# Graph attention of the last layer with nodes on partitions: row sums from ACT, squares crossed from SBUF to SBUF

## The chip, the cores and the metric

The kernel runs on one core of one Trainium2 chip. The metric is the device time of one execution in microseconds (us). Engines are named as in the profile: PE (TensorE matmul), PEld (its weight loads), DVE (VectorE), ACT (ScalarE), POOL (GpSimd), SP (SyncE, which issues nearly all DMAs).

## What is computed

The input x has 32 graphs of 512 nodes with 256 channels; all share one 512x512 adjacency. Four layers run in a row, each as x = x + layer(relu(layernorm(x))): two dense-and-attention blocks (layer 0), a graph attention with self loops (layer 1), a masked multi-head attention of 8 heads with two layer norms (layer 2), and the graph attention that this change is about (layer 3), of 4 heads with 64 channels:

```python
q = (h @ W).reshape(B, N, H, D)
e_src = jnp.einsum('bnhd,d->bnh', q, a_src)
e_dst = jnp.einsum('bnhd,d->bnh', q, a_dst)
e = e_src[:, :, None, :] + e_dst[:, None, :, :]
e = jnp.where(e >= 0, e, ALPHA * e)              # ALPHA = 0.2
e = jnp.where((adj > 0)[None, :, :, None], e, NEG_INF)
attn = jax.nn.softmax(e, axis=2)
h_prime = jnp.einsum('bijh,bjhd->bihd', attn, q)
return jax.nn.elu(h_prime.reshape(B, N, H * D))
```

A node without any neighbour gets equal weights on all nodes, so its result is the mean over all nodes.

## The kernel before

All numbers are float32. A graph's array of 512 nodes and 256 channels lies as 128 partitions x 4 blocks x 256 (a "cell", 32 of which stand in SBUF); its turned form has the channels on partitions. Up to six graphs are in flight (IN_FLIGHT), and their steps are interleaved.

The order is made when the program is built. Every step is an `Op` with an engine, an assumed length, and the buffers that it reads and writes; `Plan.order` places all steps of all graphs one by one, on each engine the step that is due first among those that can start, and hands out cells, PSUM banks, rows, pages and sheets as it goes. A step's due time comes from the rest of its graph's chain, a period per graph (PERIOD) and one number per step (SHIFTS). The result is one fixed order of instructions on each engine and on SP's DMA queue; at run time semaphores hold each instruction until its data are there, and what stands behind it on the same engine waits with it.

Layer 2 (`mha`) has nodes on partitions while it makes probabilities: PE makes scores (L1347), DVE adds the mask and takes the extreme of each row (L1367), ACT makes exponentials and their sums (L1378 with its accumulator read), DVE turns every 32x32 square in place (L1386), and the squares are then exchanged between the four groups of 32 partitions by a trip through DRAM: one store of 128 partitions to a "sheet" (L1391), four loads that each land on 32 partitions (L1399). `turned_round` turns the input of layers 0 and 2 in the same way through a "page" (`crossed`, L615 and L622; squares on DVE, L636). `transposed` (L655 on PE, L663 on ACT) turns it with PE for layers 1 and 3 and after the first norm of layer 2.

Layer 3 has the nodes that are summed over on partitions from the start (`layer3`, from L1450). For each of four heads, one after the other, `gat_probabilities` (L776) spreads three columns into rows with PE transposes of a broadcast column against the identity (`rows_ps`, L720): the neighbours' terms for the masked maximum (DVE, L791, into a scratch tile `masked`), a shift per node (four small operations on POOL, L806 to L809, and a copy on ACT, L730), and the nodes' own terms. POOL adds the shift to the turned mask (L821, two of 128x1024), DVE takes the larger of the two slopes and adds (L832), ACT makes the exponentials (L840). The leaky slope is thus a maximum on DVE, not a function on ACT. POOL adds the four blocks of probabilities (L1484, L1488), PE multiplies them with q (L1502, two heads side by side in 64 columns each), a matrix of ones makes the sums (L1523), PE turns rows back (L1539), DVE scales (L1548 to L1561). `lonely` and `spread` add the mean for nodes without neighbours (L851, L859, L870, L1572). `elu_to_xt` applies elu, fetches the residual from a page (L973) and adds it (L1222). One store of 512 KB takes the result out (L1588).

Of the kernel before, what the change touches and what calls it, by code (L numbers as in the profile page):

```python
# [39 lines left out]
FLOOR = -(2.0**60)  # L40
TINY = 1e-30
# [3 lines left out]
CELL = NC * (C + 5)  # L45
ROW = N + 10
SMALL = 320
BUFFERS = {"cell": 32, "row": 7, "page": 48, "sheet": 12}
# [6 lines left out]
PERIOD = 50.7  # L55
# [3 lines left out]
    72, 50, 37, 26, 40, 30, 9, 57, 9, 9, 9, 9, 50, 27, -10, -39, 3, -6, 21, -19, -30, -122,  # L59
    -182, -23, -9, -33, 39, 5, -2, 1, -49, 1, 1, 0, -66, 1, 1, 1, 1, -16, 1, -38, -1, -71, -1,  # L60
    0, -23, 1, 2, -22, 1, 3, 1, -103, 1, 5, 1, -19, 1, 1, 19, 1, -26, 1, -3, 1, 1, 1, 14, 5, 0,
    1, 1, -10, 1, -2, 0, 0, 0, 1, 0, -1, 0, -1, 6, 0, -115, 19, 0, 7, -25, -6, 0, -32, -35, 0,
    68, 0, 35, 0, 93, -3, 2, 24, -51, 18, -11, 0, -7, 1, -75, 1, 1, 55, 0, 26, -26, 4, 3, 0,
    -39, -1, -162, -3, -56, -2, -13, 1, -20, -2, -37, -87, -26, -9, -7, -1, -27, -9, -52, -40,
    6, -52, -18, 0, -6, -4, 2, -5, -23, -88, 0, -14, -42, 12, -11, -1, -2, 6, -7, -10, -1, -49,
    -29, -3, -1, -23, 2, 0, -84, 10, -16, -46, -3, 7, 7, -17, 0, 0, 0, 0, -18, 0, 4, 144, 2, 0,
    -3, 0, -7, 2, -24, 27, -28, 31, -92, 47, -25, -10, 1, 0, -3, 0, 109, 0, -1, -75, -1, 0, 0,
    -3, 0, -7, -45, 0, 41, -1, 2, -7, 69, -15, -49, -3, -3, 0, 22, -97, -17, 4, -12, -9, 4, -53,
    -11, -1, -1, -5, 17, 5, 72, 47, 46, 74, 146, -16, -51, 41, -3, -13, -15, 2, 0, 1, 49, -18,
    -5, 30, 3, 4, 0, 0, -1, 0, 18, 14, -12, -32, 78, -1, 37, -82, -4, 7, -6, 0, 9, -3, -12, 9,  # L70
    0, -70, 20, 0, -10, 0, -1, 0, 23, 0, 0, -33, -10, 28, 83, 95, 37, 17, 76, -5, -36, -119,
    -25, -1, 92, 3, 0, 2, -3, 0, -24, 1, 0, -10, -5, -3, -36, -2, -46, -24, -68, 25, -10, -11,
    -13, -5, -2, -29, -22, -1, -1, -13, -2, 3, 14, 0, 0, 0, 28, 7, -83, -101, 7, 46, -9, -54,
    -46, 44, -24, 99, -5, -1, 0, 0, 75, 0, 0, 0, -10, 0, 1, 6, 0, 14, 0, 23, 13, -17, 53, 6, 87,
    -7, -16, 7, 3, 5, -1, -71, -87, 15, -12, 0, 11, 0, 0, 0, 8, 0, 0, -9, -8, 0, 23, 0, 0, -80,
    2, 0, 18, 0, 0, -3, 0, 0, 105, -13, -36, -11, -81, -30, -85, -143, -51, -24, -71, -29, -116,
    -48, -84, -82, -187, -154, -123, -175, -94, -43, -87, -62, 6, -91, -111, -160, -332, -388,
    -421, -351, -608, -395, -425, -396, -421, -341, -408, -335, -348, -464, -413, -372, -375,
    -378, -330, -297, -285, -312, -291, -315, -190, -199, -193, -90, -130, -236, -99, 76, -225,
    -189, -251, -299, -395, -387, -220, -242, -187, -183, -124, -28, -137, -109, -189, -108,  # L80
    -163, -117, -33, -55, -60, -125, -183, -244, -216, -176, -221, -264, -255, -199, -296, -271,
    -259, -434, -424, -521, -444, -340, -233, -214, -298, -180, -115, -52, -68, -145, -240,
    -205, -240, -241, -326, -236, -241, -474, -309, -46, -175, -128, -162, -177, -202, -326,
# [325 lines left out]
def adj_preln_kernel(  # L409
# [83 lines left out]
    w1_sb = weights(w1, "w1_sb")  # L493
    b1_bc = column(b1, "b1_bc")
    w2_sb = weights(w2, "w2_sb")
    l3_sb = weights(W_3, "l3_sb", TERMS * GAT_HEADS)
    ln1_g_bc = column(ln1_g, "ln1_g_bc")
    ln1_b_bc = column(ln1_b, "ln1_b_bc")
    ln1_g_row = row(ln1_g, "ln1_g_row")
# [1148 lines left out]
```

## Time and profile before

| | |
|---|---|
| time, median of 3 runs | 4420.88 us (4417.97 to 4422.98) |
| the profiled execution: time, span | 4422.42 us, 4420.6 us |
| mean granted PE clock | 0.979 |
| instructions | 69,315 |
| DMA | 867 MB, 196 GB/s over the span |
| DMAs with data, issued by SP | 2,102 |
| stores of results (L1588), start of the first, the 28th, the 32nd | 571, 4097, 4417 us |

The page lists busy time by engine, the granted clock and the DMA share in 40 slices, the chain of work that ended last, and groups of instructions by line: count, busy time in us, mean ns of one, and the idle time of the engine just before them with what ended it. A window gives the busy time of each engine in a stretch, then the granted clock, the share of the 16 DMA engines' time that packets took, and GB/s. Matmuls overlap, so a matmul's own duration is longer than the time until the next one can start.

### The profile page before, as it was taken

To read this page: it belongs to the slowest core of one execution; us is meant where nothing else is said; L and a number is where in the kernel's file an instruction comes from. 1 tells how busy PE (TensorE), PEld (TensorE's weight loads), DVE (VectorE), ACT (ScalarE), POOL (GpSimd) and SP (SyncE) were. 2 spreads that over 40 slices of the span, in tenths; PEclk is the share of its full clock that TensorE was granted. 3 is DMA by queue.
4 is the path that set the end of the run, shared out by engine and by line. 5 is a ranking of instruction groups with operands and counts; after the bars stand their busy time and mean duration, and the time that the engine had idled before them with its cause. 6 is when DMAs were issued, how large, how long until landed. Compare 5 with 4: busy or idle time off the path is not lost. (4 is left out here: it accounts for less than half of the span.)

```text
span 4420.6 us, 69315 instructions
## 1 busy us (share of the span) xinstructions
PE 4170.8 (94%) x21648; PEld 2583.3 (58%) x21648; DVE 3662.7 (83%) x9016; ACT 2924.3 (66%) x6309; POOL 3034.1 (69%) x3119
## 2 busy tenths in 40 slices
PE   6999999999999999999999999999999999999765
PEld 3656556665566666566666556666656666655332
DVE  3577888888888888888888888888889888888873
ACT  2556666777676667667667767666766766676653
POOL 1424766777776677776677777667777766777677
PEclk9999999999999999999999999999999999999877
DMA  3287667766767766766777667677667677766760
GB/s 121 84 226 218 187 190 220 218 202 181 215 199 211 224 200 201 204 204 194 222 215 204 201 200 211 194 224 210 205 205 206 192 217 219 201 200 186 231 175 29
DMA packets 441504, 867.22 MB, mean 196 GB/s; under 512 B 35248, under 2 KB 119728, under 8 KB 441136
## 3 DMA queue, kind: packets, MB, share of 16 engines
q1 hardware_dynamic: 439520, 862.78, 66.4%
q8 instruction: 173, 2.83, 0.3%
q14 instruction: 195, 1.60, 0.1%
q10 hardware_dynamic: 1616, 0.01, 0.0%
HBM read 443.23 MB, written 419.43 MB: 195 GB/s over the span
## 5 line engine op out<-in xcount | busy, mean ns | idle before, releaser
L1386 DVE STREAM_TRANSPOSE cells<-cells 128x512 f32<-128x512 f32 x1024 | 702.4, 698 | 148.8 <-ACT cells L1378 148.5
L1378 ACT ACTIVATE cells<-cells,smalls 128x512 f32<-128x512 f32 x1024 | 736.1, 719 | 114.0 <-DVE smalls L1367 105.8
L1367 DVE CUSTOM_DVE_ANT_0 cells<-bank,mask_bias 128x512 f32<-128x512 f32 x1024 | 686.9, 674 | 21.6 <-PE bank L1347 20.6
L821 POOL TENSOR_TENSOR cells<-mask_biasT,row 128x1024 f32<-128x1024 bf16 x320 | 682.3, 2155 | 16.2 <-ACT row L730 16.2
L791 DVE CUSTOM_DVE_ANT_0 masked<-bank,mask_bias 128x512 f32<-128x512 f32 x768 | 520.5, 678 | 71.1 <-PE bank L720 64.7
L683 PE MATMUL bank<-cells,mlp_sb 128*128 128x512 f32 x1024 | 473.1, 600 | 19.8 <-DMA cells<-page 13.2
L704 PE MATMUL bank<-fc_sb,cells 128*128 128x256 f32 (+1 forms) x2048 | 474.7, 381 | 1.5 <-DVE smalls L1367 0.8
L927 PE MATMUL bank<-cells 128*128 128x260 f32 x2048 | 465.1, 383 | 1.1 <-ACT cells L840 0.9
L603 ACT ACTIVATE cells<-cells,smalls 128x256 f32<-128x256 f32 x768 | 408.1, 592 | 74.7 <-POOL smalls L596 49.7
L1159 PE MATMUL bank<-cells 128*128 128x512 f32 x1024 | 450.9, 597 | 0.0
L927 PEld LDWEIGHTS bank<-cells 128*128 128x128 f32 x2048 | 387.9, 190 | 87.1 <-issue 24.9
L840 ACT ACTIVATE cells<-cells,smalls 128x512 f32<-128x512 f32 x512 | 348.5, 726 | 114.7 <-DVE cells L832 114.6
L704 PEld LDWEIGHTS bank<-fc_sb,cells 128*128 128x128 f32 x2048 | 376.9, 189 | 76.5 <-DVE cells L1442 19.0
L586 DVE BATCH_NORM_STATS2 smalls<-cells 128x6 f32<-128x256 f32 x768 | 311.3, 405 | 110.4 <-POOL cells L1222 101.3
L883 ACT ACTIVATE cells<-cells 128x512 f32<-128x512 f32 (+1 forms) x256 | 188.1, 735 | 292.9 <-DVE cells L946 111.3
L832 DVE SCALAR_TENSOR_TENSOR cells<-bank,smalls,cells 128x512 f32<-128x512 f32 x512 | 354.1, 740 | 30.5 <-POOL cells L821 27.0
L720 PEld LDWEIGHTS bank<-ident,smalls 128*128 128x128 f32 x2176 | 254.3, 141 | 212.6 <-issue 84.2
L720 PE MATMUL bank<-ident,smalls 128*128 128x128 f32 x2176 | 325.9, 284 | 54.2 <-POOL smalls L809 30.0
L1159 PEld LDWEIGHTS bank<-cells 128*128 128x128 f32 x1024 | 194.1, 193 | 230.2 <-issue 228.7
L1484 POOL TENSOR_TENSOR cells<-cells 128x1024 f32<-128x1024 f32 x128 | 302.3, 2372 | 19.2 <-PE bank L1502 8.4
L683 PEld LDWEIGHTS bank<-cells,mlp_sb 128*128 128x128 f32 x1024 | 186.0, 191 | 218.5 <-issue 170.3
L1347 PE MATMUL bank<-cells 32*128 32x512 f32 x2048 | 305.8, 644 | 5.7 <-DVE smalls L1367 4.8
(141 smaller groups left out, 8503.9 us busy)
## 6 DMA issues: line engine op xcount, KB each, us to landing
sheet<-cells SPq DMA_DIRECT2D x256, 1024.0 KB, 5.3
cells<-sheet SPq DMA_DIRECT2D x1024, 256.0 KB, 5.4
page<-cells SPq DMA_DIRECT2D x256, 512.0 KB, 3.4
cells<-page SPq DMA_DIRECT2D x192, 512.0 KB, 6.1
cells<-in_x_dram SPq DMA_DIRECT2D x64, 512.0 KB, 7.3
cells<-page SPq DMA_DIRECT2D x256, 128.0 KB, 2.9
out_dram<-cells SPq DMA_DIRECT2D x32, 512.0 KB, 5.4
mlp_sb<-in_L_gnn_mlp_w_dram SPq DMA_DIRECT2D x2, 512.0 KB, 6.7
```

The source lines that it names most:

```text
L603: lambda c=c: act.activation(xn[:, c, :], src[:, c, :], func, bias=off[:, c : c + 1], scale=rstd[:, c : c + 1],),
L683: lambda k=k, s=s, i=i, m=m, mm=mm: pe.matmul(mm.ap, w[:, k, cols + m * P : cols + (m + 1) * P], s.rows(i), start=(k == 0), stop=(k == nk ...
L704: pe.matmul(mm[:, :n], src[k // 2].nodes(k % 2, c), w[:, k, cols : cols + n], start=(k == 0), stop=(k == nk - 1),)
L720: pe.transpose(bc[:, c * P : (c + 1) * P], col(c).to_broadcast([P, P]), ident)
L791: lambda c=c: dve.tensor_tensor_reduce(masked, f2_ps.ap, bias[:, c, :], 1.0 - ALPHA, FLOOR, op0=ALU.add, op1=ALU.max, accum_out=top[:, c : ...
L821: lambda half=half: pool.tensor_add(p[half].ap, biasT[:, 2 * half : 2 * half + 2, :], w_row[:, None, :].to_broadcast([P, 2, N]),),
L832: lambda j=j, ph=ph, i=i: dve.scalar_tensor_tensor(ph[:, i, :], f1_ps.ap, term(2)[:, j : j + 1], ph[:, i, :], op0=ALU.max, op1=ALU.add,),
L927: pe.matmul(mm[:, :w1], p[j // 2][:, j % 2, c * P : (c + 1) * P], v[:, j, :], start=(j == 0), stop=(j == NC - 1),)
L1159: pe.matmul(mm.ap, h1[jh][:, i, m * P : (m + 1) * P], p[jh][:, i, :], start=(jh + i == 0), stop=(jh + i == 2),)
L1367: dve.tensor_tensor_reduce(tile(), sc[h].ap.rearrange("p (j f) -> p j f", j=NC), mask_bias[:, c, :].rearrange("p (j f) -> p j f", j=NC), - ...
L1378: lambda h=h, c=c, tile=tile: act.activation(tile(), tile(), AF.Exp, scale=-1.0, bias=low[:, c, h : h + 1], accum_out=sums[:, c, h : h + 1],),
L1386: dve.transpose(squared, squared)
```

## The change

Layer 3 is made like layer 2's attention, with nodes on partitions until the probabilities are done. Its input is turned by DVE and a trip through a page (`turned_round`) in place of PE and ACT, which leaves the nodes in "square order" (the position of a node's block and its group of 32 are exchanged); the mask is brought into this order once at the start, and the residual and the result are moved in it by four DMAs each. One row per head is spread by PE (`square_row`). DVE adds the mask and takes row maxima (into the probabilities themselves), ACT applies the leaky slope (Prelu with the node's own term as bias) and the exponential with its row sum, DVE turns the squares in place. For two heads at a time, 16 DMAs of 128 KB exchange the squares straight from SBUF to SBUF, 32 partitions to 32 partitions; then PE multiplies in one step. The sums by POOL and PE, the turned mask's adds, the mean for nodes without neighbours and the third group of columns in the weights go. The mask's value is so large that a row without neighbours comes out with equal weights by itself.

Buffers change a little: five rows in place of seven, cells smaller by four columns, 342 small columns per graph in place of 320. Steps per graph go from 657 to 721 by the program's count (PE 132 to 117, ACT 158 to 170, POOL 57 to 37, DVE 181 to 182, DMAs 65 to 108). PERIOD and all SHIFTS are new, so the order of steps is new everywhere, not only in layer 3.

```diff
@@ constants
+LOWEST = -3.0e38
+PAIR = 2
 ...
-CELL = NC * (C + 5)
-ROW = N + 10
-SMALL = 320
-BUFFERS = {"cell": 32, "row": 7, "page": 48, "sheet": 12}
+CELL = NC * (C + 4)
+ROW = N + 8
+SMALL = 342
+BUFFERS = {"cell": 32, "row": 5, "page": 48, "sheet": 12}
-PERIOD = 50.7
+PERIOD = 52.0
 SHIFTS = (
...
 )
@@ new helpers
+        def square_row(self, holder, col, dst):
+            bc = Buffer("bank", N)
+            def emit():
+                for c in range(NC):
+                    pe.transpose(
+                        bc.ap.rearrange("p (q c i) -> p q c i", q=NC, i=SQUARE)[:, :, c, :],
+                        col(c).to_broadcast([P, P]),
+                        ident,
+                    )
+            self.op("pe", 0.47, holder, [bc, *dst], emit)
+            return bc
+        def masked_probabilities(self, holder, far, near, n, table, p, tile, parts, sums=None):
+            bias, key = table
+            f2_ps = self.square_row(holder, far, [p])
+            top = self.small(f"top{n}", NC)
+            m = self.small(f"m{n}", NC)
+            for c in range(NC):
+                self.op(
+                    "dve", 0.77, [f2_ps, [(key, c, q) for q in range(P // SQUARE)]], [top, parts(c)],
+                    lambda c=c: dve.tensor_tensor_reduce(
+                        tile(c),
+                        f2_ps.ap.rearrange("p (a i) -> p a i", i=tile(c).shape[2]),
+                        bias[:, c, :].rearrange("p (a i) -> p a i", i=tile(c).shape[2]),
+                        1.0, LOWEST,
+                        op0=ALU.add, op1=ALU.max, accum_out=top[:, c : c + 1],
+                    ),
+                )
+            self.op(
+                "pool", 0.35, [top, *holder], [top],
+                lambda: pool.tensor_add(top.ap, top.ap, near()),
+            )
+            def emit():
+                act.activation(m.ap, top.ap, AF.Prelu, alpha=ALPHA)
+                act.activation(m.ap, m.ap, AF.Copy, scale=-1.0)
+            self.op("act", 0.45, [top], [m], emit)
+            for c in range(NC):
+                self.op(
+                    "act", 0.72, [*holder, parts(c)], [parts(c)],
+                    lambda c=c: act.activation(
+                        tile(c), tile(c), AF.Prelu, bias=near()[:, c : c + 1], alpha=ALPHA
+                    ),
+                )
+            for c in range(NC):
+                def emit(c=c):
+                    out = {} if sums is None else {"accum_out": sums[0](c)}
+                    act.activation(tile(c), tile(c), AF.Exp, bias=m[:, c : c + 1], **out)
+                self.op(
+                    "act", 0.72 if sums is None else 0.82, [m, parts(c)],
+                    [parts(c), *([sums[1]] if sums else [])], emit,
+                )
+                def emit(c=c):
+                    squared = tile(c).rearrange("p a (l i) -> p a l i", i=SQUARE)
+                    dve.transpose(squared, squared)
+                self.op("dve", 0.69, [parts(c)], [parts(c)], emit)
+        def squares_crossed(self, src, dst, read, write, kbytes):
+            squares = P // SQUARE
+            for turn in range(squares):
+                for l in range(squares):
+                    to = (l + turn) % squares
+                    def emit(l=l, to=to):
+                        nc.sync.dma_start(
+                            dst(slice(to * SQUARE, (to + 1) * SQUARE), l),
+                            src(slice(l * SQUARE, (l + 1) * SQUARE), to),
+                        )
+                    self.transfer([read], write(l, to), kbytes, emit, True, 0.6)
@@ the residual, fetched in square order
+        def fetched_squares(self, page, after):
+            dst = Buffer("cell", *page.shape)
+            for q in range(P // SQUARE):
+                def emit(q=q):
+                    nc.sync.dma_start(
+                        dst[q * SQUARE : (q + 1) * SQUARE],
+                        page[:, q, :].rearrange("(c i) f -> i c f", i=SQUARE),
+                    )
+                self.transfer(
+                    [page, *after], [[(dst, "from", q)]], 128, emit, True
+                )
+            return dst
@@ share(): the mask in square order, once
+            quarters = range(P // SQUARE)
+            page = [("mask page", 0)]
+            self.transfer(
+                [[("mask", c) for c in range(NC)]], [page], 256,
+                lambda: nc.sync.dma_start(mask_page, mask_bias),
+            )
+            for q in quarters:
+                def emit(q=q):
+                    nc.sync.dma_start(
+                        mask_square[q * SQUARE : (q + 1) * SQUARE],
+                        mask_page[:, q, :].rearrange("(c i) f -> i c f", i=SQUARE),
+                    )
+                self.transfer(
+                    [page], [[("square", c, q) for c in range(NC)]], 64, emit, True
+                )
@@ the residual added
-        def add_to_xt(self, y, after):
-            xt = self.fetched(self.x_page, after)
+        def add_to_xt(self, y, after, squares=False):
+            xt = (self.fetched_squares if squares else self.fetched)(self.x_page, after)
+            landed = [(xt, "from", q) for q in range(P // SQUARE)]
             for g in range(2):
                 s = slice(2 * g, 2 * g + 2)
                 self.op(
-                    "pool", 1.42, [xt.part(2 * g, 2), y.part(2 * g, 2)], [xt.part(2 * g, 2)],
+                    "pool", 1.42, [xt.part(2 * g, 2), y.part(2 * g, 2), landed],
+                    [xt.part(2 * g, 2)],
                     lambda s=s: pool.tensor_add(xt[:, s, :], xt[:, s, :], y[:, s, :]),
                 )
             self.xt = xt
-        def elu_to_xt(self, y, after):
+        def elu_to_xt(self, y, after, squares=False):
             for g in range(2):
                 s = slice(2 * g, 2 * g + 2)
                 self.elu(lambda s=s: y[:, s, :], y.part(2 * g, 2), (2, C))
-            self.add_to_xt(y, after)
+            self.add_to_xt(y, after, squares)
@@ layer3
             xn = self.normalized(self.xt, AF.Relu, 1)
-            hT = self.transposed(xn)
...
+            hT = self.turned_round(xn)
+            v = Buffer("cell", NC, C)
+            f = self.small("f8", NC, PAIR, GAT_HEADS)
+            n = C + PAIR * GAT_HEADS
             for c in range(NC):
                 mm = Buffer("bank", N)
...
+                self.nodes_first([hT], l3_sb, 0, n, c, mm, v.part(c))
                 def emit(c=c, mm=mm):
                     act.activation(
                         f[:, c, :, :].rearrange("p t h -> p (t h)"), mm[:, C:n], AF.Copy
                     )
...
-            mean = self.lonely(q, C)
...
+                    act.activation(v[:, c, :], mm[:, :C], AF.Copy)
+                self.op("act", 0.57, [mm], [f, v.part(c)], emit)
+            sums = self.small("sumh", NC, GAT_HEADS)
+            rinv = self.small("rinvh", NC, GAT_HEADS)
+            z = Buffer("cell", NC, C)
             for g in range(GAT_HEADS // 2):
...
+                p = Quad(NC, 2, NC, P)
+                pT = Quad(NC, 2, NC, P)
                 for i in range(2):
                     h = 2 * g + i
-                    p, top = self.gat_probabilities(
...
+                    self.masked_probabilities(
+                        [f], lambda c, h=h: f[:, c, 0, h : h + 1], lambda h=h: f[:, :, 1, h],
+                        f" of {i}", (mask_square, "square"), p,
+                        lambda c, p=p, i=i: p[:, :, i, c, :],
+                        lambda c, p=p, i=i: [(p, i, c)],
+                        (lambda c, h=h: sums[:, c, h : h + 1], sums),
                     )
...
-                sums.append(total)
+                self.squares_crossed(
+                    lambda at, to, p=p: p[at, to].rearrange("p h c i -> p (h c i)"),
+                    lambda at, l, pT=pT: pT[at, l].rearrange("p h c i -> p (h c i)"),
+                    [(p, i, c) for i in range(2) for c in range(NC)],
+                    lambda l, to, pT=pT: [[(pT, l, to)]],
+                    128,
+                )
                 acc = Buffer("bank", N)
                 r = Buffer("row", N)
...
+                def emit(g=g, pT=pT, acc=acc):
+                    for j in range(NC):
+                        for i in range(2):
+                            d = (2 * g + i) * GAT_DIM
+                            pe.matmul(
+                                acc[i * GAT_DIM : (i + 1) * GAT_DIM, :],
+                                v[:, j, d : d + GAT_DIM],
+                                pT[:, :, i, :, j * SQUARE : (j + 1) * SQUARE].rearrange(
+                                    "p l c i -> p c l i"
+                                ),
+                                start=(j == 0),
+                                stop=(j == NC - 1),
+                            )
+                squares = [(pT, l, to) for l in range(NC) for to in range(P // SQUARE)]
+                self.op("pe", 3.5, [v, squares], [acc, r], emit)
                 self.op(
                     "act", 0.6, [acc], [r],
                     lambda acc=acc, r=r: act.activation(r.ap, acc.ap, AF.Copy),
                 )
...
                 back = Buffer("bank", NC, P)
                 def emit(r=r, back=back):
                     for c in range(NC):
                         pe.transpose(back[:, c, :], r[:, c * P : (c + 1) * P], ident)
...
-            self.spread(mean, y)
...
+                self.op("pe", 0.5, [r, z], [back], emit)
                 def emit(g=g, back=back):
+                    hs = slice(2 * g, 2 * g + 2)
+                    dve.reciprocal(rinv[:, :, hs], sums[:, :, hs])
                     dve.tensor_mul(
                         z[:, :, g * P : (g + 1) * P].rearrange("p c (h d) -> p c h d", h=2),
                         back.ap.rearrange("p c (h d) -> p c h d", h=2),
...
+                        rinv[:, :, hs, None].to_broadcast([P, NC, 2, GAT_DIM]),
                     )
...
-            self.elu_to_xt(z, [rows[1]])
+                self.op("dve", 0.9, [back, sums], [rinv, z], emit)
+            self.elu_to_xt(z, [z.part(0)], True)
@@ build(): the result stored
-            self.transfer([res], [], 512, lambda: nc.sync.dma_start(out_v[i], res.ap))
-            plan.writers["left", i] = [plan.ops[-1]]
+            rows_v = out[i].rearrange("(q c i) f -> q i c f", q=NC, i=SQUARE)
+            stores = []
+            for q in range(P // SQUARE):
+                self.transfer(
+                    [res], [], 128,
+                    lambda q=q: nc.sync.dma_start(
+                        rows_v[q], res[q * SQUARE : (q + 1) * SQUARE]
+                    ),
+                )
+                stores += plan.ops[-2:]
+            plan.writers["left", i] = stores
```

## The prediction

> **What bounds the kernel now.** I read the page's busy shares first, then the windows of equal length, because the shares average a start, a long even middle and a tail.
>
> ```profile
> span 4420.6 us, 69315 instructions
> PE 4170.8 (94%) x21648; PEld 2583.3 (58%) x21648; DVE 3662.7 (83%) x9016; ACT 2924.3 (66%) x6309; POOL 3034.1 (69%) x3119
> ```
>
> ```profile
> 1200.00:1800.00 600.00, 591.30 (x3148) 371.64 (x3147) 524.04 (x1290) 414.45 (x904) 429.66 (x447) 1.00 0.72 211
> 3000.00:3600.00 600.00, 590.19 (x3100) 372.44 (x3100) 522.78 (x1278) 418.28 (x917) 431.36 (x440) 1.00 0.71 209
> 4250.00:4421.00 171.00, 100.97 (x444) 52.46 (x442) 86.20 (x204) 72.58 (x136) 135.23 (x129) 0.78 0.24 70
> ```
>
> In the middle PE is busy 590 of 600 us at full clock: PE sets the pace, and DVE (523) is second. In the last 171 us POOL is the busiest (135) and PE waits. The stores of the results start at 571 us (first) and 4097 us (28th), so the middle runs at (4097 - 571) / 27 = 130.6 us per graph, and the time is 571 + 27 x 130.6 + 324 of tail. Five windows from 600 to 3600 us give per graph (their sums over 3000 us, times 130.6): PE 128.1, DVE 114.0, ACT 90.8, POOL 94.9, and DMA at a share of 0.70 91.4.
>
> A busy PE is not work at its peak, so I take PE's prices from starts, not from the means of one instruction:
>
> ```profile
> 2033.45 1.04 PE L720 MATMUL bank<-ident,smalls 128*128 128x128 f32 x8
> 2034.33 5.35 PE L704 MATMUL bank<-fc_sb,cells 128*128 128x256 f32 x24
> ```
>
> The next group starts 0.88 us after eight transposes, so one costs 0.11 us, where its mean in the groups by line says 0.28. Those groups carry the other prices:
>
> ```profile
> L1378 ACT ACTIVATE cells<-cells,smalls 128x512 f32<-128x512 f32 x1024 | 736.1, 719 | 114.0 <-DVE smalls L1367 105.8
> L1386 DVE STREAM_TRANSPOSE cells<-cells 128x512 f32<-128x512 f32 x1024 | 702.4, 698 | 148.8 <-ACT cells L1378 148.5
> L821 POOL TENSOR_TENSOR cells<-mask_biasT,row 128x1024 f32<-128x1024 bf16 x320 | 682.3, 2155 | 16.2 <-ACT row L730 16.2
> L832 DVE SCALAR_TENSOR_TENSOR cells<-bank,smalls,cells 128x512 f32<-128x512 f32 x512 | 354.1, 740 | 30.5 <-POOL cells L821 27.0
> L720 PE MATMUL bank<-ident,smalls 128*128 128x128 f32 x2176 | 325.9, 284 | 54.2 <-POOL smalls L809 30.0
> L1484 POOL TENSOR_TENSOR cells<-cells 128x1024 f32<-128x1024 f32 x128 | 302.3, 2372 | 19.2 <-PE bank L1502 8.4
> L1378 ACT ACTIVATION_READ_ACCUMULATOR cells<-cells,smalls 128x1 f32 x1024 | 199.8, 195 | 0.0
> ```
>
> **PE, on the path.** Per graph the last layer loses two of three row broadcasts per head: 4 heads x 2 x 4 transposes = 32 at 0.11 = 3.5 us (at 0.127, the group's start-to-start mean without idle, 4.1). The transposed input goes to DVE: 8 at 0.11 = 0.9. The sums by a matrix of ones (L1523) cost 1.2 us by their starts, their turning back (four of L1539) 0.4, the column mean (L859) 0.45. The product with the probabilities keeps its 32 instructions; it now reads its moving side in runs of 32, as L1412 does: 61 ns each, four column tiles side by side, so 244 ns for 256 columns against L927's 220 for 260. I take it as unchanged; it may gain some 0.25 us from one block in place of two, or lose 0.5. The sixteen transposes that stay write four runs of 32 columns each, which no row shows from PE: L720 is nearest, so 0.11 again, at worst twice that (1.8 us more). Sum: 4.2 to 7.3, I take 6.7. PE falls from 128.1 to 121.4 us per graph.
>
> **POOL, beside the path in the middle.** Per head go two adds of L821 (4.3), one of L1484 (2.4), one of L1488 (1.4) and three of four small ones (0.8); per graph the column mean, its spreading and adding (2.0 + 1.9 + 2.9). That is 35.6 + 6.8 = 42 of 94.9: POOL drops to 53 us. In the chain of waits of the last 220 us L821 has 12.3%, the most of any line, and L1484 7.8%: the last layer's part of these leaves it.
>
> **DVE, nearly even.** Sixteen of L832 go (11.9), sixteen transposes come (11.2), two more turn the input (1.4), and the small operations on the sums nearly cancel. The masked maxima stay: they write into the probabilities instead of a scratch tile, which L1367 does in 674 ns against L791's 678. Net +0.7, to 114.7. Against this, L896's 128x512 takes 890 ns and its 128x1024 only 1249, so some of DVE's time looks like waiting; with less POOL up to 1.5 us per graph may come back. [...]
>
> **ACT.** Sixteen Prelu at 0.72 (L1378 and L840's 0.726: in place, with a bias column) are 11.5 us; sixteen accumulator reads at 0.195 are 3.1; eight small ones at 0.21 are 1.7. Out go four row copies, two of the transposed input, the sums' and the mean's: 4.5. ACT rises by 11.8 to 102.6. Prelu stays in the one loaded table: the changed program still has a single table load, as now (1283 ns, once).
>
> **DMA, the new load.** 43 more issues per graph. The input's turn is known: 128 packets of 4 KB at 161 ns and 512 of 1 KB at 56 ns, over 16 engines 1.3 + 1.8 us; the residual's fetch in 1 KB runs adds 0.3. The two crossings are 1024 packets of 4 KB. No transfer from SBUF to SBUF is in the trace. I bound it by packet records: alone in flight, a 4 KB packet to or from all partitions takes 158 to 162 ns; the 2 KB packets of the stores to the sheets (all partitions) take 86, those of the loads from them, which land on 32 partitions each, 142, at worst 173. The crossings have 32 partitions at both ends, so I take 162 x 142 / 86 = 267 ns: 17.1 us. Bounds: 162 ns gives 10.4, twice 158 gives 20.2. DMA becomes 91.4 + 3.4 + 17.1 = 112 us per graph (105 to 115).
>
> [...]
>
> **SP** issues at a pace of 0.48 us (L1399's median), so a crossing holds it for 16 x 0.48 = 7.7 us, with other graphs' stores to the sheets (L1391) behind it. All 43 add some 20 us per graph to the 32 that it issues now (1034 us over 32 graphs), far from full.
>
> **The sum.** PE stays the longest, 121.4, but DVE (114.7) and DMA (112) now stand within 8% of it, where only DVE did. In the middle PE was 98% busy; I take 96%, because PE's product now waits for sixteen landings, and every other graph's matmul that stands behind it in PE's order waits too: 121.4 / 0.96 = 126.4. That PE idles more is an estimate; its ends are 98% (123.8) and the old pace (130.6). The start gains little, 8 us. In the tail POOL's 42 us per graph leave the chain, but the last graph gains two round trips (page, crossing) of some 10 us each: I take -20, ends -45 and 0. So 563 + 27 x 126.4 + 304 = 4280 us of span, 4282 with the 1.8 us around it (4422.4 profiled, 4420.9 median: no correction).
>
> **Rivals.** (1) PE stays as dense as now, since in every 123.8 us DVE is still free for 9, DMA for 12 and ACT for 21: 123.8 per graph, 563 + 3343 + 290 = 4196. For it: PE's idle time of 10 us in 600 shows that six graphs in flight cover what waits there are. Against it: DMA had 30% slack and keeps 11%. (2) Slower: the DMA engines become the bound. One place, the crossings; one price, 20.2 us (every packet twice 158 ns), so 115 per graph; decisive once the engines can't be kept above a share of 115 / 132 = 0.87 on average, since the old time with a 20 us shorter tail is reached at 131.6 per graph. The best 50 us window of the trace reaches 0.89, most 0.71. At 0.85 it is 135.3 per graph: 563 + 3653 + 324 = 4540. Against it: 20 us windows reach 1.05 (packets overlap), so 0.89 may be demand, not a ceiling. The sign is this:
>
> ```profile
> cells<-sheet SPq DMA_DIRECT2D x1024, 256.0 KB, 5.4
> page<-cells SPq DMA_DIRECT2D x256, 512.0 KB, 3.4
> ```
>
> these landings would grow beyond 7 us. (3) The saving on PE turns wholly into waits: DVE and DMA near 90% with fixed orders on every queue hold the pace at 130 to 131.6: 4380 to 4420.
>
> **How the numbers follow.** My case (125 to 129 per graph, 4225 to 4350) gets 0.48, (1) 0.24, (3) 0.16, (2) 0.12. Differences under 0.2%, 9 us, are what a measurement of this kernel can't tell from none. Of (3), 0.05 falls within that and 0.11 is faster: faster 0.83, same 0.05, slower 0.12. The range leaves out (2), part of (3) and the end of (1): 4190 to 4395.
>
> **What would show it.** Right: per graph PE at 121 to 122 us with a share of 0.95 to 0.97 in the middle, L832 and L821 fewer by half or more, POOL under 45% of the span, DMA share 0.85 to 0.9, stores some 126 us apart. The 4 KB packets of the crossings show their own price: 267 ns or not. Wrong: stores more than 130 us apart, PE idle before the product or before L1412 because of DMA, landings of the sheets beyond 7 us; or, the other way, PE as dense as now.

## The result: 9.5% slower, and the profile after

The changed kernel takes 4843.1 us (median of 4 runs, 4836.5 to 4849.4) against 4421.9 us: a ratio of 1.0953, interval 1.0931 to 1.0975. The forecast was 4282 us.

The page and three windows of the changed kernel: 600 us of the middle, all of the middle, and the end (busy us of each engine with its number of instructions, then PE's granted clock, the DMA engines' share, GB/s):

```profile
span 4847.6 us, 67524 instructions
PE 4157.7 (86%) x19920; PEld 2485.0 (51%) x19920; DVE 3691.9 (76%) x9078; ACT 3188.7 (66%) x7333; POOL 1705.9 (35%) x2063
```

```profile
1200.00:1800.00 600.00, 535.85 (x2601) 320.58 (x2600) 480.05 (x1159) 417.72 (x957) 218.98 (x262) 0.95 0.80 223
600.00:3600.00 3000.00, 2672.08 (x12920) 1600.47 (x12919) 2389.10 (x5847) 2064.93 (x4757) 1110.71 (x1335) 0.94 0.79 223
4250.00:4848.00 598.00, 397.65 (x1838) 214.22 (x1838) 395.43 (x995) 355.03 (x845) 165.01 (x207) 0.81 0.73 197
```

POOL is relieved as meant. But no engine is full any more: PE was busy 590 of 600 us at full clock and is now busy 536 at 0.95. Over the 3000 us of the middle it idles 328 us, where it idled 58. The stores of the results start at 589 us (first) and 4480 us (28th): 144.1 us per graph in place of 130.6. Where PE idles, its two groups of products show (busy us, mean ns of one, then the idle time before the group and what ended most of it), and the list of PE's waits says how often (us in total, times, longest). The third line is of the kernel before, where layer 2's product is L1412:

```profile
L1526 PE MATMUL bank<-cells 128*32 128x256 f32 x4096 | 351.7, 502 | 309.1 <-DMA cells<-sheet 168.1
L1610 PE MATMUL bank<-cells 128*64 128x512 f32 x1024 | 314.6, 770 | 158.4 <-DMA cells<-cells 108.1
L1412 PE MATMUL bank<-cells 128*32 128x256 f32 x4096 | 258.8, 395 | 32.6 <-DMA cells<-sheet 13.7 <-issue 7.5 <-DVE cells L1386 7.4
```

```profile
PE bank L1526 <- DMA cells<-sheet: 168.1, 36, 8.1
PE bank L1610 <- DMA cells<-cells: 108.1, 22, 18.4
```

L1526 is layer 2's product, which the change does not touch. L1610 is the last layer's (L1502 before: 11.3 us of idle time, 622 ns). Of its 108 us of waits for crossings 24 fall between 600 us and the 28th store, and 76 in the tail behind it. The issues that these wait for, with the median us to landing:

```profile
sheet<-cells SPq DMA_DIRECT2D x256, 1024.0 KB, 6.5
cells<-sheet SPq DMA_DIRECT2D x1024, 256.0 KB, 6.4
page<-cells SPq DMA_DIRECT2D x288, 512.0 KB, 5.2
cells<-cells SPq DMA_DIRECT2D x1024, 128.0 KB, 2.4
```

A load from a sheet lands 1.0 us later than before, a store to a page 1.8. From the end of a set's transposes to its last load landed (steps matched in order of time), the sheet trip has a median of 20.5 us where it had 13.7.

One thing adds to the price of a wait. Two stretches of PE in the timeline (start, duration, operation, count), and the granted clock over them:

```profile
2483.66 0.60 PE L857 MATMUL bank<-ident,smalls 128*128 128x128 f32 x4
2489.16 3.64 PE L1526 MATMUL bank<-cells 128*32 128x256 f32 x32 [4.90 <-DMA cells<-sheet]
...
2515.00 1.93 PE L1526 MATMUL bank<-cells 128*32 128x256 f32 x32
```

```profile
2487.28:2494.11 6.83, 4.95 (x34) 2.41 (x35) 2.74 (x10) 1.26 (x3) 0.41 (x2) 0.50 1.04 376
2515.00:2516.93 1.93, 1.93 (x37) 1.00 (x36) 1.90 (x3) 1.40 (x3) 0.77 (x2) 1.00 0.88 197
```

After 4.90 us of waiting the same 32 matmuls take 3.64 us in place of 1.93, at a clock of 0.50. Between 600 and 4000 us the records of the granted clock hold 73 such stretches of 3.4 or 6.8 us, 389 us together; the kernel before has 4 with 14 us. Of the 73, 48 began at a gap of 2.9 to 5.7 us in PE's work. The other 25 had no gap above 2.1 us, only shorter ones that left PE idle for 1.0 to 2.0 of the 3.4 us before.

### The profile page after: what moved, and what is told of

Same layout as the page of the kernel before. It is cut to its first block, busy times and chain, and to the rows that moved or that the text cites. A ratio compares the mean times of both kernels' runs of the same rounds, so it can differ in the third digit from the quotient of the medians.

```text
span 4847.6 us, 67524 instructions
## 1 busy us (share of the span) xinstructions
PE 4157.7 (86%) x19920; PEld 2485.0 (51%) x19920; DVE 3691.9 (76%) x9078; ACT 3188.7 (66%) x7333; POOL 1705.9 (35%) x2063
## 5 line engine op out<-in xcount | busy, mean ns | idle before, releaser
L1492 ACT ACTIVATE cells<-cells,smalls 128x512 f32<-128x512 f32 x1024 | 733.7, 717 | 520.6 <-DVE smalls L1481 520.1
L1500 DVE STREAM_TRANSPOSE cells<-cells 128x512 f32<-128x512 f32 x1024 | 705.4, 698 | 93.2 <-ACT cells L1492 93.0
L1526 PE MATMUL bank<-cells 128*32 128x256 f32 x4096 | 351.7, 502 | 309.1 <-DMA cells<-sheet 168.1
L598 POOL TENSOR_TENSOR smalls<-smalls,eps 128x4 f32<-128x4 f32 x192 | 39.2, 204 | 1298.7 <-DVE smalls L592 1176.0
L983 DVE SCALAR_TENSOR_TENSOR cells<-cells 128x512 f32<-128x512 f32 (+1 forms) x256 | 323.8, 1267 | 185.0 <-ACT cells L979 167.2
L1610 PE MATMUL bank<-cells 128*64 128x512 f32 x1024 | 314.6, 770 | 158.4 <-DMA cells<-cells 108.1
L1014 PEld LDWEIGHTS bank<-cells 128*128 128x128 f32 x2048 | 386.4, 191 | 81.6 <-issue 18.0
L914 DVE STREAM_TRANSPOSE cells<-cells 128x512 f32<-128x512 f32 x512 | 340.7, 693 | 96.1 <-ACT cells L905 92.8
L1526 PEld LDWEIGHTS bank<-cells 128*32 128x32 f32 x4096 | 162.5, 138 | 475.1 <-issue 298.1
L897 ACT ACTIVATE cells<-cells,smalls 128x512 f32<-128x512 f32 x512 | 350.7, 711 | 44.4 <-DVE smalls L875 40.9
L905 ACT ACTIVATE cells<-cells,smalls 128x512 f32<-128x512 f32 x512 | 362.1, 708 | 0.0
L875 DVE CUSTOM_DVE_ANT_0 cells<-bank,mask_square 128x512 f32<-128x512 f32 x512 | 330.8, 675 | 15.0 <-PE bank L857 10.8
L837 DVE SCALAR_TENSOR_TENSOR cells<-bank,cells 128x512 f32<-128x512 f32 x256 | 178.6, 735 | 191.1 <-DMA cells<-sheet 108.1
```

Source lines behind the costliest of these rows:

```text
L897: lambda c=c: act.activation(tile(c), tile(c), AF.Prelu, bias=near()[:, c : c + 1], alpha=ALPHA),
L905: act.activation(tile(c), tile(c), AF.Exp, bias=m[:, c : c + 1], **out)
L1014: pe.matmul(mm[:, :w1], p[j // 2][:, j % 2, c * P : (c + 1) * P], v[:, j, :], start=(j == 0), stop=(j == NC - 1),)
L1492: lambda h=h, c=c, tile=tile: act.activation(tile(), tile(), AF.Exp, scale=-1.0, bias=low[:, c, h : h + 1], accum_out=sums[:, c, h : h + 1],),
L1500: dve.transpose(squared, squared)
L1526: pe.matmul(acc[d, :], v[:, j, g * P + d.start : g * P + d.stop], pT[:, :, :, h, j * SQUARE : (j + 1) * SQUARE].rearrange("p l c i -> p c l i"
```

## The experiments

Ratios are to the kernel before, measured beside each group of runs (its median is 4414 to 4424 us). Differences in us are to the changed kernel's 4843.1 us, or, for versions of the kernel before, to that kernel. First comes the crossing, four ways, then the order, then the landings and DVE beside POOL, and last other orders of the same steps.

### The crossing: issues, bytes, place

**Four issues in place of 16.** Only the last turn of each group of 32 partitions issues, and moves all that partitions hold:

```diff
-                            dst(slice(to * SQUARE, (to + 1) * SQUARE), l),
-                            src(slice(l * SQUARE, (l + 1) * SQUARE), to),
+                            if turn < squares - 1: return
+                            # 512 KB: all of a group of 32 partitions onto another group
```

> The changed kernel, its order of steps untouched, with each crossing made by 4 issues of 512 KB in place of 16 of 128 KB: the same bytes, still from 32 partitions to 32 others, but whole groups instead of the right squares (this leaves out the exchange itself, so the values are not the reference's). Theory 'queue' (32 issues of 0.63 us per graph hold SP, and the sheets of layer 2 behind them come late): below 4600 us. Theory 'bytes' (the packets between 32 and 32 partitions, 284 ns each, slow every other transfer): 4800 to 4850. Theory 'order' (the new order of all steps is slower by itself): 4750 or more.

4819.7 us, 1.0901 (1.0856 to 1.0947): 23 us less, which fits both 'bytes' and 'order'. Fewer issues with the same bytes gain little. This doesn't price the issues alone, since each of the four lands after 7.7 us, where one of the sixteen landed after 2.4.

**An eighth of the bytes**, 16 issues:

```diff
-                            dst(slice(to * SQUARE, (to + 1) * SQUARE), l),
-                            src(slice(l * SQUARE, (l + 1) * SQUARE), to),
+                            dst(slice(to * SQUARE, (to + 1) * SQUARE), l)[:, :128],
+                            src(slice(l * SQUARE, (l + 1) * SQUARE), to)[:, :128],
```

> The changed kernel with 16 issues per crossing as before, each moving 512 bytes per partition in place of 4 KB (an eighth of the bytes; most probabilities are left uncrossed). 'Queue': 4750 to 4850, since the issues stay. 'Bytes': below 4500, DMA share in the middle under 0.70. 'Order': 4750 or more.

4726.4 us, 1.0690 (1.0655 to 1.0726): 117 us less, 3.7 us per graph for about 15 us of DMA time. None of the three theories had this: it is 24 us below 'queue' and 'order', and far above 'bytes'.

**No crossing.** The DMAs go, and PE multiplies the probabilities as they lie:

```diff
-                        nc.sync.dma_start(...)
+                        return
-                def emit(g=g, pT=pT, acc=acc):
+                def emit(g=g, pT=p, acc=acc):
```

> The changed kernel without the crossings: no issue, no bytes, PE multiplies with the uncrossed squares as soon as they are turned; the order of all other steps is the same. 'Queue' and 'bytes' both: 4200 to 4400, the crossing is what costs. 'Order': above 4600, the slow pace stays without any crossing.

4627.8 us, 1.0467 (1.0426 to 1.0509): 215 us less. Half of the loss stays with no crossing at all. From an eighth of the bytes to none is 99 us, about as much as the other seven eighths: the 32 issues per graph with their landings cost too, and no run parts the one from the other. PE still waits for the sheets of layer 2, for 141 us (L1523 is L1526; line numbers move by a few with the edits, here and below):

```profile
PE bank L1523 <- DMA cells<-sheet: 141.5, 31, 12.4
```

**Through DRAM**: one store of 2 MB per crossing and four loads of 512 KB, as layer 2 does it, in the places of the old issues.

```diff
+     ways = [[pages.tile([P, QUAD], FP, ...) for g in range(2)] for k in range(IN_FLIGHT)]
-     16 transfers of 128 KB, cells to cells
+     the first issue: all of p to a way; the last four: a way to 32 partitions of pT each
```

> The changed kernel with the crossing undone to layer 2's way: one store of 2 MB to DRAM and four loads of 512 KB that land on 32 partitions each, in the places of the 16 direct transfers (the result is complete). 10 issues per graph in place of 32, but twice the bytes (8.4 MB) and a wait for the store on SP. 'Queue': 4600 to 4800, unless SP's wait for the store takes back what the issues gave. 'Bytes': 4950 or more. 'Order': 4800 to 4900.

5125.9 us, 1.1594 (1.1558 to 1.1630): 283 us more. Placed in this order, straight from SBUF to SBUF is the cheaper way.

### The order: shifts taken away

`SHIFTS = ()` in both kernels, so that each is planned from its due times alone; and the kernel before with its own shifts for the last layer and the changed kernel's for layers 0 to 2.

> The kernel before with SHIFTS empty, so that due times come from each step's own chain and the period alone; nothing else is changed. It shows what the numbers in SHIFTS are worth for the old last layer. Theory 'structure' (the new last layer can't be interleaved as densely, whatever the numbers): 4450 to 4750, and below the changed kernel treated in the same way by 5% or more. Theory 'order' (the changed kernel is slow by its new numbers): 4450 to 4750 too, but not below the changed kernel treated in the same way.

> The changed kernel with SHIFTS empty. 'Structure': slower than the kernel before with SHIFTS empty by 5% or more, 4850 to 5100. 'Order': no slower than the kernel before with SHIFTS empty, and not above the changed kernel's 4843.

> The kernel before, its own numbers for layer 3 and the store kept, with the changed kernel's numbers for the steps of layers 0 to 2 (which are the same steps in both). 'Order': these numbers carry the loss, 4650 to 4850. 'Structure': within 3% of the kernel before, 4420 to 4550.

| | without shifts | with its shifts |
|---|---|---|
| before | 4687.4, 1.0610 (1.0571 to 1.0650) | 4421 |
| after | 4832.3, 1.0939 (1.0897 to 1.0980) | 4843 |

The kernel before with the other's shifts in layers 0 to 2 takes 4995.4 us, 1.1308 (1.1263 to 1.1352), beyond the 4850 expected; it is a mixture that nobody fitted as a whole, so it shows how much shifts can cost and no more. The old shifts are worth 6% to the old kernel, and the new ones are worth nothing to the changed kernel. Without shifts the two are 145 us (3.1%) apart, with them 422. Neither theory had that: 'structure' asked for 5% or more, 'order' for no distance. So the new layer 3 costs something in these orders too, but most of the loss is an order that fits the chip in one kernel and not in the other.

### What the new order waits for: landings and DVE beside POOL

**Half of each sheet transfer** left out from the seventh graph on, in both kernels:

```diff
+            half = PACK * P // (2 if self.i >= IN_FLIGHT else 1)
-                            sheet[:, :, c % 2, :],
+                            sheet[:, :, c % 2, :half],        # and the loads alike
```

> The changed kernel in its own order, with every store to and load from the sheets in layer 2 cut to half its bytes from the seventh graph on (the other half is left out; all instructions stay). Layer 2 is not touched by the change, so this asks what the new order waits for. 'Landings' (the new order runs layer 2's round trips with no slack, so that each us by which a landing is late is paid): removing about 28 us of DMA time per graph brings the landings forward and takes 220 to 280 us off, 4560 to 4620 us, with PE's wait ahead of the MHA product mostly gone. 'Multiplying instructions' (the new layer 3 itself, its issues and waits, is what costs): layer 2's transfers are off the path, 4800 us or more.

> The kernel before with the same cut of the sheet transfers, the control of the run above. 'Landings': the old order has slack there, so it gains at most 60 us, 4360 us or more. If transfers bound both kernels alike, it gains as much as the changed kernel does (220 us or more, about 4200 us).

After: 4542.6 us, 1.0275 (1.0253 to 1.0296), 300 us less, somewhat more than 'landings' had. Before: 4377.5 us, 0.9898 (0.9882 to 0.9915), 47 us less, as expected. Layer 2 is the same in both, and shorter trips are worth six times as much to the new order. Changed kernel, then the kernel before, both with half sheets:

```profile
600.00:3600.00 3000.00, 2796.23 (x13924) 1697.16 (x13923) 2575.85 (x6298) 2213.67 (x5123) 1191.51 (x1430) 0.97 0.65 186
```

```profile
600.00:3600.00 3000.00, 2955.93 (x15667) 1841.64 (x15668) 2642.23 (x6483) 2107.30 (x4564) 2200.13 (x2258) 1.00 0.48 151
```

In the changed kernel PE's wait for sheets falls from 168 to 29 us, and the stretches at half clock from 389 to 181 us:

```profile
PE bank L1527 <- DMA cells<-sheet: 29.0, 6, 8.2
```

**POOL's adds cut to 8 columns** (L1287, L1336, L1420), the order as it was:

```diff
-                    lambda s=s: pool.tensor_add(xt[:, s, :], xt[:, s, :], y[:, s, :]),
+                    lambda s=s: pool.tensor_add(xt[:, s, :8], xt[:, s, :8], y[:, s, :8]),
```

> The changed kernel in its own order, with three kinds of POOL instructions (the additions onto x, the addition of the residual in layer 0 and the multiplication by the second norm's weights) cut to 8 of their columns, the rest left out. These are the ones that run when VectorE's elu instruction with two SBUF inputs is slow. 'Lock' (DVE's instructions held up by POOL's set the pace): the elu instructions go from a mean of 1123 ns to about 650, 3 to 5 us per graph, 4680 to 4750 us. 'Landings': DVE has room, the instructions get shorter and the time stays within 30 us of 4843 us.

4719.9 us, 1.0673 (1.0657 to 1.0689): 123 us less. The groups by shape of DVE's elu instruction, which reads two SBUF operands; the changed kernel, then this one:

```profile
L983 DVE SCALAR_TENSOR_TENSOR cells<-cells 128x512 f32<-128x512 f32 x192 | 215.2, 1123 | 134.9 <-ACT cells L979 117.1 <-ACT cells L974 17.8
L983 DVE SCALAR_TENSOR_TENSOR cells<-cells 128x1024 f32<-128x1024 f32 x64 | 108.6, 1698 | 50.1 <-ACT cells L979 50.1
```

```profile
L983 DVE SCALAR_TENSOR_TENSOR cells<-cells 128x512 f32<-128x512 f32 x192 | 132.8, 693 | 150.2 <-ACT cells L979 124.2 <-ACT cells L974 26.0
L983 DVE SCALAR_TENSOR_TENSOR cells<-cells 128x1024 f32<-128x1024 f32 x64 | 78.4, 1224 | 49.9 <-ACT cells L979 49.9
```

Per graph that is 6 x 0.43 + 2 x 0.47 = 3.5 us less on DVE, and 123 / 32 = 3.8 us less time, though DVE is busy only 80% of the middle. The adds themselves are shorter too, which this run does not separate from the shorter elu instructions. Of the changed kernel's 192 with 512 columns 59 take over a fifth longer than the shortest, and each of them overlaps a POOL instruction; 102 of the others overlap none, and 31 overlap one without being that long. With the adds cut a single one is that long. The prediction expected that "with less POOL up to 1.5 us per graph may come back". Instead their mean went from 890 ns in the kernel before to 1123 ns: 59 instructions are long where by the same measure 68 were, but the slowest tenth is beyond 2530 ns in place of 1327. All of that tenth overlap POOL's long addition L1287 (2.36 us).

### Other orders of the same steps

The planner was run with other shifts, every step, transfer and buffer as in the change. Each order was replayed with the durations and landings of the measured profile, and the shifts were searched for an early end of the replay.

```diff
-SHIFTS = (118, 32, -87, ...)
+SHIFTS = (...)          # found by the search; two runs of it
```

> The changed kernel with every instruction, transfer and buffer as it is; only the numbers that shift the due times are others. They were searched for so that the planned order, replayed with the durations and landings that the profile of the changed kernel shows instead of the planner's own, ends early; the replay puts this order 285 us ahead of the changed kernel's. 'Landings' (the cost is that the new order was placed with transfers that land sooner than they do): 4480 to 4680 us. 'The new layer 3 costs by itself' (its transfers, its waits, PE's lower clock, in any order): within 60 us of 4843 us.

> The same with another set of numbers from another start of the same search (replay: 278 us ahead of the changed kernel's order). 'Landings': 4480 to 4680 us, within 60 us of the run above. 'The new layer 3 costs by itself': within 60 us of 4843 us.

4635.0 us, 1.0481 (1.0463 to 1.0498), and 4686.9 us, 1.0599 (1.0573 to 1.0625), the latter 7 us beyond what was expected. The first takes 208 us off with nothing but the order, and the second 156. In the first the wait for sheets falls from 168 to 56 us; the trip itself shortens from 20.5 to 17.4 us, though a single load lands no sooner (6.8 us). In the second the wait for sheets does not fall, and the gain is spread over other waits: from 600 to 3600 us PE idles 267 us there, 215 in the first and 328 in the given order. So the sheets are one of the places where the given order waits, not the only one. The lines are PE's waits in the first order, then in the second:

```profile
PE bank L1616 <- DMA cells<-cells: 74.7, 6, 21.6
...
PE bank L1532 <- DMA cells<-sheet: 56.5, 31, 9.3
```

```profile
PE bank L1532 <- DMA cells<-sheet: 166.9, 31, 12.0
```

DVE's delay beside POOL is not what the first order removes: the elu instructions with 512 columns have a mean of 1138 ns there, and 1123 in the given order.

A third order was planned with later landings from the start, and its shifts were searched from zero:

```diff
-        def transfer(self, reads, writes, kbytes, emit, load=False, issue=0.45, lag=2.2):
-            self.op("dma", kbytes / RATE, reads, writes, lambda: None, lag if load else 1.0)
+        def transfer(self, reads, writes, kbytes, emit, load=False, issue=0.45, lag=4.0):
+            self.op("dma", kbytes / RATE, reads, writes, lambda: None, lag if load else 3.0)
-RATE = 290.0; PERIOD = 52.0
+RATE = 250.0; PERIOD = 54.0          # the new figures rounded
```

> The changed kernel with all its steps, planned with other prices: a transfer lands 4.0 us after its bytes (3.0 for a store) where the planner had 2.2 and 1.0, the rate is 250 in place of 290, the period 54, and the shifts were searched anew from zero. The replay puts this order 20 us ahead of the first other order (4635 us). 'Landings': 4560 to 4680 us, that is, an order made for the real landings wins some 200 us, and no more is to be had by order alone. 'The shifts are what counts, not the landings': an order that starts from no shifts stays near the run without shifts, 4780 to 4850 us.

4611.4 us, 1.0438 (1.0422 to 1.0455). Three orders that know the landings end within 76 us of each other, 156 to 232 us ahead of the given one. In this third one PE is busy 575 of 600 us, and DMA reaches 0.86. Its sheet trips are no shorter than in the given order (a median of 21.8 us), and PE hardly waits for them any more:

```profile
1200.00:1800.00 600.00, 574.90 (x2780) 347.13 (x2781) 500.50 (x1259) 445.81 (x1027) 239.05 (x282) 0.96 0.86 238
```

```profile
PE bank L1528 <- DMA cells<-sheet: 12.3, 3, 10.0
```

**What is left in the better order.** The first other order without the crossings, and with half sheets besides:

> The first other order (4635 us) without the crossings of the last layer: their 32 DMAs per graph are left out and PE multiplies the probabilities as they stand before the crossing. If the crossings and the given order were one cost (the order failed only because of the crossings' landings), leaving them out now gains little: 4580 us or more. If they are a cost by themselves, the gain is as large as in the given order (4843 to 4628 us): 4400 to 4460 us, about the time of the kernel before.

> As the run above, and layer 2's sheet transfers cut to half their bytes as well (from the seventh graph on). DMA has some 70 us per graph left. If PE's term of the prediction (121.4 us per graph) is right and only transfers stood between it and the time, PE is then busy over 95% of the middle: 4230 to 4340 us. If the new layer 3 holds PE in another way (DVE and ACT with more in one chain), it stays above 4400 us.

4465.5 us, 1.0104 (1.0084 to 1.0124): the crossings cost 170 us here, so they cost by themselves, though the result is a little above what was expected. With half sheets 4428.5 us, 1.0025 (1.0016 to 1.0035). That is not the 4230 to 4340 of transfers alone, but the other case of the expectation, that the new layer 3 holds PE in another way. Stores start 131.6 us apart, with DMA at half its share, and PE waits for rows that ACT and DVE prepare:

```profile
1200.00:1800.00 600.00, 570.40 (x2877) 350.82 (x2874) 520.69 (x1279) 451.94 (x1045) 235.99 (x287) 0.97 0.47 147
```

```profile
PE bank L1553 <- ACT row L1545: 80.7, 35, 8.0
PE bank L1553 <- DVE smalls L1485: 30.5, 27, 1.2
```

The order was searched for long landings and was not searched again for short ones, so this run can't say how close to 121.4 us per graph the new layer 3 could come.

**The control**, the kernel before with the same search:

> The control: the kernel before, all its steps as they are, with shifts found by the same search on the same replay (which puts this order 77 us ahead of the old one). The old order keeps PE busy 98% of the middle, so at most 2% is there to win: 4350 to 4425 us. If it gained 200 us as the changed kernel did, the search would be the cause and not the mismatch of the new order.

4391.2 us, 0.9941 (0.9924 to 0.9958). The search (which moved the planner's rate, period and lags by under 2% as well) finds 27 us there, not 208: the old order was already near what the search can find, and the new one was not. More than 2% was not to be had with PE busy 98%, so this control can't tell what the search would win on an unfitted order of the old steps; that was not run. This is the fastest of all versions run: the old steps in another order, PE busy 592 of 600 us.

```profile
1200.00:1800.00 600.00, 592.00 (x3143) 371.07 (x3142) 531.62 (x1299) 418.67 (x916) 433.34 (x455) 1.00 0.71 208
```

## Why the prediction was wrong

**The work was about right.** From the window of 600 to 3600 us at 144.1 us per graph:

| per graph, us | predicted | measured |
|---|---|---|
| POOL | 53 | 53.4 |
| DVE | 114.7 | 114.8 |
| ACT | 102.6 | 99.2 |
| DMA, share times period | 112 | 114 |
| a crossing's 4 KB packet, ns | 267 | 284 (alone in flight, mean) |
| PE | 121.4 | 128.3 busy, at the least 121.5 at full clock |

PE's last figure takes off the most that the half clock can have cost. PE is busy in 321 of the 389 us of those stretches, and half of that is 160 of 3400 us, or 6.8 us per graph. The run without crossings in the better order gives 122.3 in the same way (2832 / 3000 x 132.0 less 2.3). At 284 ns the packets of the two crossings take 18.2 us per graph, where the prediction had 17.1.

**The step that failed** is "In the middle PE was 98% busy; I take 96%", with "98% (123.8) and the old pace (130.6)" as its ends. PE was 89% busy, and part of that at half clock. With the measured period the sum reads 589 + 27 x 144.1 + 368 = 4848, against 563 + 27 x 126.4 + 304: 478 us of the 568 us of error lie in the middle, 26 at the start and 64 in the tail. In the middle that is 17.7 us per graph: the sum allowed 5.0 us of idle time and PE idled 15.8, and it counted 121.4 us of work where PE was busy 128.3, which the half clock nearly covers (up to 6.8). The sum had nothing for the clock. In the tail it gave the crossing and the page some 10 us each and expected 20 us less in all; PE waits 76 us for crossings there. Nothing in the profile made the old pace an end: it was the pace of an order that had been fitted, and every number of that order was new. The working has a term for each step that the change adds and none for the order, although the text of the change says that PERIOD and all SHIFTS are new. The runs price it: 208 us with the first other order, 232 with the third, and 6% is what fitted shifts are worth to the kernel before.

**Waits add up where there is no slack.** The prediction took from the old profile that six graphs in flight cover the waits. In the old order they do: half sheets change it by 47 us. In the new order three excesses are paid: trips that end later (300 us less with half sheets), DVE held up beside POOL (at most the 123 us with POOL's adds cut, which also shortens the adds), and PE's clock behind its waits (at most 160 us). The three overlap and are not to be added.

**The half clock was missed.** After a wait of 4.9 us the product behind it took 1.7 us more, at a clock of 0.50. The stretches at this clock last 3.4 or 6.8 us (up to 13.7 in the third other order) and their starts lie multiples of 3.41 us apart. Not each of them follows a long wait: 25 of the 73 began without any gap above 2.1 us, and what set those off stays open. At most 160 us, under 5% of the middle, is the price here. The better orders keep most of it: 328 us run at half clock in the first and 297 in the third. No run took the half clock away alone, so this share is read from the clock's records, not shown by an experiment.

**SP** issued a crossing at 0.634 us per DMA, not 0.48: 10.1 us per crossing in place of 7.7. Four issues in place of 16 gained 23 us, with later landings against them.

**The rivals.** (1), PE as dense as now, is out. (3) had the mechanism, savings turned into waits, and the wrong end. (2) is nearest in sign but not in cause: it had the DMA engines at a ceiling. In the middle the share stands at 0.79, and the third other order runs it at 0.86 with a shorter period, so 0.79 was no ceiling; its sign, sheet landings beyond 7 us, did not come (6.4 and 6.5). The runs point not to a shortage of transfers but to transfers that the order expected earlier: the planner counts 2.2 us behind a load's bytes and 1.0 behind a store's. The old kernel was planned with the same figures, and its order still leaves room for the landings. Why the new shifts fit badly stays open: no run shows how either set was found.

**Of the 422 us**, then, 208 are the order and 170 the crossings in the better order. Taken the other way round, the crossings are 215 and the order 162, so the split depends on which goes first. The rest, some 45 us (4465 against 4421), is not settled, and neither is whether an order exists in which the new layer 3 comes out ahead; the best that was found took 4611 us with the crossings and 4465 without.

## What to carry to other kernels

Where the order of instructions is fixed when the program is built, a change of steps is two changes, and the new order wants its own price: ask with which landings and durations it was planned, compare these with the profile, and take the worth of the old fit (run it without) as the size of what can be lost. An engine that is 98% busy says nothing on how much slack the others have behind it; halving one transfer in both kernels shows that for the price of two runs. And idle time of TensorE was paid for a second time here, in the slower clock behind it: 1.7 us after a wait of 4.9, at a granted clock of 0.50 in place of 1.00.

## What the runs showed of the hardware

- Prelu with a bias column per partition and a slope costs ACT 711 ns for 128x512 (L897), as much as the exponential beside it (708 ns, L905), with one table load (1283 ns) in the whole program.
- A DMA of 32 partitions x 4 KB from SBUF to SBUF holds SP 590 ns (median), where a load of 256 KB from DRAM onto 32 partitions holds it 430; its median to landing is 2.4 us.
- The exchange of squares through DRAM in place of SBUF to SBUF was worse in the same order, 5126 against 4843 us, with DMA at 0.82 and 237 GB/s in the window from 1200 to 1800 us.
